# Attention and a mixture of experts on one core: the last second-turn expert is picked on the chip, and half of the final layer norm moves in among the last expert slots

## The chip, the cores and the metric

The kernel runs on one core of a Trainium2 chip. The metric is the time of one execution on the device in microseconds (us). The kernel before the change was timed three times; the median is compared.

## The reference

Input `x` is 4 x 1024 x 256 in float32. Two layers follow each other, each with a residual and a layer norm without weights:

```python
x = layernorm(x + attention(x))      # 16 heads of 16, causal, latent projections, rope
x = layernorm(x + x_moe)             # written out below, x_moe = experts' output plus x
```

The second layer sends every token to 2 of 8 experts:

```python
scores = (x @ router_w.T + router_b) / temp          # per token, 8 experts
gates = sinkhorn(scores, iters=3)                    # over experts, then over the tokens of one element
topk_gates, topk_idx = top_k(gates, 2)               # gates divided by their sum
out_e = (relu(x @ wg[e]) * (x @ wp[e])) @ wo[e]      # 256 -> 512 -> 256
x_moe = x + sum over the two experts of gate * out_e
```

The Sinkhorn step normalizes over the tokens of one element of the batch, so routing can go element by element. There are 4 x 1024 x 2 = 8192 pairs of a token and an expert, on average 1024 to an expert.

## The kernel before

**Attention and routing.** The four elements of the batch are attended one after the other. While element `b` is attended, `finish(b - 1)` makes the first layer norm of the element before and writes its rows to two tensors in DRAM: `x1_rows`, from which the experts gather, and `results`, onto which the experts' outputs are added. `route(b - 1)` (L682) then works out the gates, the two experts of each token, and the place of each pair. Each expert has a region of `REGION` rows in the DRAM tensor `pairs`; `base` (one column for each expert) holds where the next pair of each goes, and grows with every element routed (L824). `scatter` (L839) writes the pairs there by indirect DMAs. `lay_out` (L863) works out, after the last element, which expert has pairs beyond the first 1024, and so what the further slots work on.

**Expert slots.** Experts work in slots of up to 512 pairs (`ER`). `first` holds one slot for each expert, pairs 0 to 511 of its region. They take pairs of the first three elements alone, so that they can run while the last element is finished and routed. `second` holds one slot for each expert, pairs 512 to 1023, in reverse order of the experts. The first of these has `like` set to the last of the first turn (L1102): the same expert, so it takes over its split weights. `further` are slots of 256 pairs (`SR`) for what is left; which expert and which rows they work on is a value in SBUF that SP loads into a register (`value`, L904). `SURE = 3` of them always run; if more are filled, the rest run in a conditional block (L1223).

**One slot.** `pairs_of` (L931) loads the list of pairs, `gather` (L950) the rows of x by four indirect DMAs on GpSimd (two for a further slot), `weights` (L961) the three matrices of 512 KB on SP's queue, `halves` (L975) splits each matrix into a high and a low part (cast on ScalarE, subtraction on VectorE, two of each for a matrix), and `rows` (L986) transposes the gathered rows on PE and splits them. `slot` (L995) then does, for each of four blocks of the 512 hidden columns, the two products on PE (three passes each, for the split), relu on ScalarE, the product on VectorE, and its split. After that come the products with `wo`, for each 128 pairs one output block `eo`, which ScalarE scales by the gate (L1026) and GpSimd adds onto `results` by an indirect DMA (L1027). There are 6 buffers for `eo`. The adds of one slot wait until those of the slot before have landed, since both may touch a row. `begin` (L1191) prepares the slot after while one runs: list and gather of the slot after next, rows and splits of the next one, weights of the slot after next.

A scheduler orders the instructions of each engine when the kernel is built, by priority and by a simulated timeline. On the chip each engine works its queue in that order.

**The final layer norm.** It stands behind the last slot. SP loads `results` back in eight chunks `z` of 512 rows (L1240). For each, VectorE takes the statistics (L1254, L1255), GpSimd makes scale and offset (L1257 to L1261), and then ScalarE scales the first five (L1264) and VectorE the last three (`DZ = 3`, L1272). SP stores (L1243).

## Time and profile before

| | us |
|---|---|
| median of three runs | 1103.58 |
| lowest and highest of them | 1100.23 and 1110.93 |
| the profiled execution | 1094.58 |
| its span, first to last instruction | 1092.8 |

Busy time in the profiled execution: PE (matmul) 978.1 us, VectorE 733.1, ScalarE 625.0, GpSimd 474.4. In the profile's names, PE is TensorE, DVE VectorE, ACT ScalarE, POOL GpSimd and SP SyncE. L1027 is line 1027 of the kernel before. A line of a group gives engine, line, operation, what it writes and reads, and the count. "Idle before" is the time in which the engine stood still ahead of an instruction, with what released it. The profile's rows have the duration of an indirect DMA on POOL as the time that POOL is held, not the transfer's.

### The profile page before, as it was taken

How to read it: one execution, taken by the hardware profiler on the slowest of the kernel's cores; microseconds unless marked ns; L12 is line 12 of the kernel's file. 1: busy time of each engine (PE TensorE's matmuls, PEld its weight loads, DVE VectorE, ACT ScalarE, POOL GpSimd, SP SyncE). 2: the span in 40 equal slices, each digit the busy share in tenths (PEclk: the TensorE clock that was granted, in tenths of full speed). 3: DMA queues.
4: the chain of work that ended last, by engine and by line, in shares of the span. 5: the costliest groups of instructions: out<-in, count | busy, mean ns of one | idle time of the engine just before them, and what ended most of it. 6: DMA issues, size and time to landing. Idle time of an engine off the chain costs nothing.

```text
span 1092.8 us, 18055 instructions
## 1 busy us (share of the span) xinstructions
PE 978.1 (90%) x6436; PEld 609.1 (56%) x6436; DVE 733.1 (67%) x1622; ACT 625.0 (57%) x1314; POOL 474.4 (43%) x543
## 2 busy tenths in 40 slices
PE   6689999999999999998989996899999699999960
PEld 4555433455535355543444343478888488888860
DVE  4767787888888778677648882266675354655636
ACT  3445766766665655675556663675654355655633
POOL 6267511122443531452233216425566864654535
PEclk9889999999999999999989999899999799999995
DMA  6673420231240330333243320256563555655647
GB/s 248 182 213 103 117 96 23 63 116 52 76 121 24 100 117 3 126 82 86 58 102 84 57 71 2 80 168 162 120 169 69 128 99 137 151 144 114 148 62 308
DMA packets 71363, 119.67 MB, mean 110 GB/s; under 512 B 16416, under 2 KB 43040, under 8 KB 70880
## 3 DMA queue, kind: packets, MB, share of 16 engines
q1 hardware_dynamic: 48544, 81.76, 24.4%
q0 software_dynamic: 20672, 36.41, 15.3%
q8 instruction: 53, 0.87, 0.3%
q10 hardware_dynamic: 2048, 0.27, 0.2%
q14 instruction: 46, 0.38, 0.1%
HBM read 82.52 MB, written 35.60 MB: 108 GB/s over the span
## 4 chain that ended last, share of the span: by engine, by line
PE 76%; DVE 6%; ACT 6%; DMA 5%; issue 2%; SPq 2%; another core or an unknown queue 2%; POOL 1%; ACTq 0%; DVEq 0%; POOLq 0%
PE y L435 13%; PE s L351 11%; PE sT L455 11%; PE gp L196 3%; PE gp L197 3%; PE gp L195 3%; PE eo L195 3%; ACT pT L466 3%; PE eo L196 3%; PE eo L197 3%; PE po L622 3%; PE lp L197 2%; PE lp L196 2%; PE lp L195 2%; PE s L368 2%
## 5 line engine op out<-in xcount | busy, mean ns | idle before, releaser
L466 ACT ACTIVATE pT<-sT 128x512 f32<-128x512 f32 (+1 forms) x608 | 326.6, 576 | 183.3 <-PE sT L455 124.3
L372 DVE TENSOR_REDUCE mx<-s 128x1 f32<-128x384 f32 (+3 forms) x352 | 216.8, 633 | 43.0 <-PE s L368 36.8
L455 PE MATMUL sT<-qs,ks 98*128 98x512 bf16 (+3 forms) x768 | 216.2, 330 | 27.2 <-ACT pT L466 20.6
L351 PE MATMUL s<-ks,qs 96*128 96x512 bf16 (+3 forms) x768 | 211.9, 333 | 17.1 <-DMA ks<-parts 7.0
L381 DVE TENSOR_REDUCE mx<-s 128x1 f32<-128x512 f32 x256 | 171.4, 682 | 42.6 <-PE s L351 38.8
L473 POOL TENSOR_SCALAR_AFFINE_SELECT pT<-pT 128x512 f32<-128x512 f32 x112 | 70.5, 636 | 298.0 <-ACT pT L466 293.5
L435 PE MATMUL y<-pT,va 128*32 128x512 f32 (+3 forms) x1536 | 169.9, 502 | 2.0 <-POOL pT L473 1.3
L1027 POOL DMA_INDIRECT results<-eo,ents x64 | 104.2, 1629 | 88.2 <-ACT eo L1026 73.1
L351 PEld LDWEIGHTS <-qs 96*128 96x128 bf16 x768 | 70.9, 100 | 117.0 <-issue 89.9
L455 PEld LDWEIGHTS <-ks 98*128 98x128 bf16 x768 | 69.7, 99 | 93.1 <-issue 60.1
L195 PE MATMUL eo<-wh,hh 128*128 128x256 f32 x280 | 81.4, 292 | 7.8 <-ACT eo L1026 7.8
L189 DVE TENSOR_TENSOR wl<-w,wh 128x512 fp32r<-128x512 f32 x108 | 69.7, 684 | 27.0 <-ACT wh L188 19.3
L368 PE MATMUL s<-mask,ident_b 128*128 128x128 bf16 (+2 forms) x352 | 87.0, 248 | 0.0
L1010 DVE TENSOR_TENSOR relu<-relu,lp 128x512 f32<-128x512 f32 x64 | 43.7, 684 | 61.5 <-ACT relu L1009 21.9
L953 POOL DMA_INDIRECT xg<-x_rows,ents x64 | 65.4, 1022 | 32.8 <-issue 17.3
L196 PE MATMUL eo<-wl,hh 128*128 128x256 f32 x280 | 79.5, 285 | 0.0
L1009 ACT ACTIVATE relu<-gp 128x512 f32<-128x512 f32 (+1 forms) x76 | 42.8, 563 | 61.7 <-PE gp L197 30.8
L197 PE MATMUL eo<-wh,hl 128*128 128x256 f32 x280 | 77.8, 284 | 0.0
L845 POOL DMA_INDIRECT pairs<-ent,so_i x64 | 66.1, 1033 | 19.3 <-issue 17.6
L189 DVE TENSOR_TENSOR hl<-relu,hh 128x512 fp32r<-128x512 f32 (+1 forms) x76 | 48.5, 645 | 28.7 <-ACT hh L188 20.3
L435 PEld LDWEIGHTS y<-pT,va 128*32 128x32 f32 x1536 | 31.9, 108 | 63.3 <-issue 48.0
L195 PE MATMUL gp<-xh,wh 128*128 128x512 f32 (+1 forms) x176 | 64.3, 372 | 2.9 <-DVE relu L1010 1.8
(213 smaller groups left out, 1862.5 us busy)
## 6 DMA issues: line engine op xcount, KB each, us to landing
ks<-parts SPq DMA_DIRECT2D x90, 128.0 KB
w<-in_wg_dram SPq DMA_DIRECT2D x18, 512.0 KB
w<-in_wp_dram SPq DMA_DIRECT2D x18, 512.0 KB
w<-in_wo_dram SPq DMA_DIRECT2D x18, 512.0 KB
qs<-parts SPq DMA_DIRECT2D x66, 128.0 KB
parts<-lv POOLq DMA_DIRECT2D x12, 384.0 KB
parts<-lv POOLq DMA_DIRECT2D x24, 192.0 KB
xh<-in_x_t_dram SPq DMA_DIRECT2D x8, 512.0 KB
```

Of the source, the lines that this page charges most:

```text
L189: (sub or nc.vector).tensor_tensor(lo, src, hi.bitcast(F32), ALU.subtract)
L195: nc.tensor.matmul(ps, lhsT=sh, rhs=mh, start=(i == 0), stop=False)
L196: nc.tensor.matmul(ps, lhsT=sh, rhs=ml, start=False, stop=False)
L197: nc.tensor.matmul(ps, lhsT=sl, rhs=mh, start=False, stop=(i == n - 1))
L351: nc.tensor.matmul(ps, lhsT=q(h, half)[:NROW, t * P : (t + 1) * P], rhs=k(h, kc)[:NROW, :w], start=first, stop=last,)
L368: nc.tensor.matmul(each[:, :, w - P :], lhsT=ident_b, rhs=mask.unsqueeze(1).to_broadcast([P, m, P]), start=False, stop=True,)
L372: nc.vector.tensor_reduce(mx_of[:, half, h0 : h0 + m, t], each, AX.X, ALU.max)
L381: nc.vector.tensor_reduce(mx_of[:, kc, h, t : t + 1], ps, AX.X, ALU.max)
L435: nc.tensor.matmul(acc[g, qc][SLOT * h : SLOT * (h + 1), lo:], lhsT=va[b % 2][:, kb, at : at + SLOT], rhs=pT[:, h, lo:], start=(kb == 0), ...
L455: nc.tensor.matmul(st[:, h % m * w : (h % m + 1) * w], lhsT=k(h, kb // BPQ)[: NROW + 2, kb % BPQ * P : (kb % BPQ + 1) * P], rhs=q(h, qc)[: ...
L466: nc.scalar.activation(pT[:, h + 1 - m : h + 1, lo:], st[:, : m * w].rearrange("p (h t) -> p h t", t=w), AF.Exp, scale=scale,)
L1027: ins = nc.gpsimd.indirect_dma_start(out=results[:, :], out_offset=bass.IndirectOffsetOnAxis(ap=k.ent[:, j, 1:2], axis=0), in_=eo, in_offs ...
```

## The change

- In the routing of the second element, `order_of_second` finds the expert that has the fewest pairs of the first two elements (the lowest number among equals). The second turn runs round the experts so that this one comes last. Its slots take list and weights by registers, as the further slots do. The sharing of weights between the last first and the first second slot goes.
- The mean over the experts of pairs of the first two elements is 512, so the fewest is at most 512, and the last second slot holds none of them. When the slot before it has been added, the rows of these two elements are final, unless some expert has over 1024 pairs of them. For that case `again` raises `filled`, and the conditional block also does the norm of these rows over.
- `load_early` puts the loads of the first four chunks of z on GpSimd's queue, ahead of the output products of the last second slot. Their layer norm is issued behind the last split (`mark`) of the three further slots: two chunks, one, and one. They use buffers of the attention that are free by then.
- Behind the last slot stand chunks 4 to 7. Two of them are scaled on ScalarE and two on VectorE (`DZ = 2`).

```diff
-DZ = 3
+DZ = 2
...
+    EARLY = B // 2
...
         nc.vector.tensor_tensor(base, base, ps[:, NE : NE + E], ALU.add)
+        if b == EARLY - 1:
+            order_of_second()
...
+    def order_of_second():
+        few = tab("few", [E])
+        nc.vector.tensor_tensor(few, floor[:1], base[:1], ALU.subtract)
+        most, again = tab("most", [1]), tab("again", [1])
+        nc.vector.tensor_reduce(most, few, AX.X, ALU.min)
+        nc.vector.tensor_scalar(again, most, -float(ER), float(NOVER), ALU.is_lt, ALU.mult)
+        tables["again"] = again
+        nc.vector.tensor_reduce(most, few, AX.X, ALU.max)
+        nc.vector.tensor_scalar(few, few, most, None, ALU.is_equal)
+        nc.vector.tensor_tensor(few, few, rank[:1], ALU.mult)
+        nc.vector.tensor_reduce(most, few, AX.X, ALU.max)
+        seq = tab("seq", [2, E])
+        seqi = tables["second"] = small.tile([1, 2, E], I32, tag="seqi", name="seqi", bufs=1)
+        nc.vector.tensor_scalar(seq[:, 0], slot_no[:, :E], most, float(E + 1), ALU.subtract, ALU.add)
+        nc.vector.tensor_copy(seqi[:, 0], seq[:, 0])
+        nc.vector.tensor_single_scalar(seqi[:, 0], seqi[:, 0], E - 1, ALU.bitwise_and)
+        nc.vector.tensor_copy(seq[:, 0], seqi[:, 0])
+        nc.vector.tensor_scalar(seq[:, 1], seq[:, 0], float(REGION), float(ER), ALU.mult, ALU.add)
+        nc.vector.tensor_copy(seqi[:, 1], seq[:, 1])
...
     def pairs_of(k):
-        if k.which == 2:
-            row = value(1, k.s, NLIST - SR)
+        if k.which:
+            row = value(k.table, 1, k.s, NLIST - k.rows)
...
     def weights(k, i):
-        if k.like is not None:
-            return
-        if k.which == 2:
+        if k.which:
             if i == 0:
-                k.e = value(0, k.s, E - 1)
+                k.e = value(k.table, 0, k.s, E - 1)
...
     def halves(k, i):
-        if k.like is not None:
-            k.hl[i] = k.like.hl[i]
-            return
...
-            split(hh, hlo, r)
+            k.mark = split(hh, hlo, r)
             hs.append((hh, hlo))
             next(between, None)
+        if ahead is not None:
+            ahead()
...
-    second = [Slot(1, e) for e in reversed(range(E))]
-    second[0].like = first[-1]
+    second = [Slot(1, n) for n in range(E)]
...
+    n_early = EARLY * T // QC
+    early_z = {}
+    def load_early():
+        for i in range(n_early):
+            z = work.tile([P, T], F32, tag="yT0", name=f"ze{i}", bufs=2) if i < 2 else work.tile(
+                [P, BPQ, C], F32, tag="x1", name=f"ze{i}", bufs=X1_BUFS
+            )
+            z = early_z[i] = z.rearrange("p (n c) -> p n c", c=C) if i < 2 else z
+            with tc.issue_after(further[0].gathered.ins):
+                ins = nc.gpsimd.dma_start(out=z, in_=rows_of(results, i))
+            for o in added:
+                after(ins, o)
+
+    def run(keys, given=(), ahead={}, behind={}):
         drain(begin(keys, 0, given))
         for n, key in enumerate(keys):
-            slot(key, begin(keys, n + 1, given))
-    run(first + second + further[:SURE], (0,))
+            slot(key, begin(keys, n + 1, given), ahead.get(n))
+            for i in behind.get(n, ()):
+                with tc.issue_after(key.mark.ins):
+                    by_scalar(i, early_z[i], "e")
+
+    keys = first + second + further[:SURE]
+    n = keys.index(second[-1])
+    run(keys, (0,), {n: load_early}, {n + 1: (0, 1), n + 2: (2,), n + 3: range(3, n_early)})
...
-    for i in range(n_z):
-        load_z(i)
+    for i in range(n_early, n_z):
+        zs[i] = zp.tile([P, BPQ, C], F32, tag="z", name=f"z{i}", bufs=n_z - n_early)
+        nc.sync.dma_start(out=zs[i], in_=rows_of(results, i))
+    for i in range(n_early, n_z):
         if i < n_z - DZ:
-            for j in range(BPQ):
-                nc.scalar.activation(
-                    z[:, j, :], z[:, j, :], AF.Identity, bias=off[:, j : j + 1], scale=rstd[:, j : j + 1]
-                )
-            store_z(i, z)
+            by_scalar(i, zs[i], "f")
         else:
-            rest.append((i, z, rstd, off))
+            rest.append((i, zs[i], *norm_z(i, zs[i], "f")))
```

`by_scalar` and `norm_z` hold the same instructions as the loop of the final norm before: statistics, GpSimd's scale and offset, four activations, a store.

## The prediction

> **What bounds the kernel now.** I read the page for the share of each engine, then the windows of the last 230 us, then the rows behind the last expert, then SP's and POOL's rows.
>
> ```profile
> PE 978.1 (90%) x6436; PEld 609.1 (56%) x6436; DVE 733.1 (67%) x1622; ACT 625.0 (57%) x1314; POOL 474.4 (43%) x543
> ...
> PE   6689999999999999998989996899999699999960
> ...
> DMA  6673420231240330333243320256563555655647
> ```
>
> The page: PE is busy 90% of the span, and of its 40 slices (27.3 us each, in tenths) only the last is empty, with the DMA engines at seven tenths there.
>
> ```profile
> core 0: us, PE busy (x) PEld busy (x) DVE busy (x) ACT busy (x) POOL busy (x), PEclk, DMA share, GB/s
> 895.00:1038.00 143.00, 141.00 (x855) 124.41 (x854) 81.82 (x135) 83.49 (x168) 77.25 (x59) 1.00 0.59 138
> 1038.00:1058.00 20.00, 19.09 (x158) 18.68 (x156) 9.00 (x22) 10.04 (x26) 7.97 (x5) 1.00 0.42 66
> 1058.00:1067.00 9.00, 0.00 (x0) 0.00 (x0) 0.00 (x0) 0.16 (x1) 3.08 (x2) 0.69 0.33 40
> 1067.00:1093.00 26.00, 0.00 (x0) 0.00 (x0) 17.04 (x76) 10.04 (x20) 13.70 (x32) 0.50 0.83 323
> ```
>
> The windows (length, busy us with counts, granted clock, DMA share, GB/s) show two bounds. In the second turn of the experts, 895 to 1038 us, PE is busy 141.0 of 143 us, VectorE and ScalarE 82 and 83; in the further slots, to 1058, PE has 19.1 of 20 and the others half. Then PE has nothing: the last adds land, and 26 us of final layer norm follow.
>
> ```profile
> 1067.04 4.08 SPq L1240 DMA_DIRECT2D z<-results  x8
> 1070.39 1.41 DVE L1254 BATCH_NORM_STATS2 bnst_f<-z 128x6 f32<-128x256 f32 x4 [15.98 <-DMA z<-results]
> ...
> 1072.49 1.04 POOL L1258 TENSOR_TENSOR rstd_f<-rstd_f,neg_half 128x4 f32<-128x4 f32 x1
> ...
> 1074.18 2.07 ACT L1264 ACTIVATE z<-z,off_f,rstd_f 128x256 f32<-128x256 f32 x4 [16.02 <-POOL off_f L1261]
> ...
> 1087.98 1.38 DVE L1272 TENSOR_SCALAR z<-z,rstd_f,off_f 128x256 f32<-128x256 f32 x4 [0.67 <-POOL off_f L1261]
> ```
>
> These rows of the end are merged by line. A z chunk costs VectorE 1.57 us (four statistics of 0.41 us, their aggregates between), GpSimd 1.9 us (1.04 for the power at L1258), and 2.07 us on ScalarE or 1.38 us on VectorE to scale. GpSimd does its eight from 1072.17 to 1087.94 without a gap, and sets the end: the last store is issued at 1089.4, the span ends at 1092.8.
>
> **The change part by part.** The profiled execution took 1094.58 us (1.8 around its span), 9.0 below the median of the runs, 1103.58. The sum is made against 1094.58 and carried to the median.
>
> *1. The tail.* Four chunks stand behind the last add in place of eight. Statistics begin at 1070.4, 1072.0, 1074.1 and 1075.7, as the first four did; the fourth's end at 1077.3, GpSimd has its offset at 1080.2 as now, VectorE scales until 1081.6 (1.38), and the last store takes its 3.4 us: 1085.0. **Gain 7.8 us**; 6.5 if the fourth load lands a chunk's 1.3 us later, 9 if the last store is quicker with half as many ahead of it.
>
> *2. The order, worked out on the chip.* Thirteen small VectorE instructions in the routing of the second element (its base update ran at 509.3), one more in the layout. The layout's own rows take 0.14 to 0.16 us and start 0.19 apart in a chain: 2.5 us. Near 509 PE was busy 8.7 to 10.0 of 10 us, VectorE 5.0 to 8.6, which hides most. 0 to 2.5; I take 0.5, near the free end because VectorE has gaps.
>
> *3. Fresh weights for the first second slot*, which shared the split weights of the last first slot: 1.5 MB, 6 casts of 0.62 us on ScalarE (3.7), 6 subtractions of 0.69 us on VectorE (4.1). Between 863 and 895 these engines were busy 14.8 and 15.0 of 32 us: 0, and 4.1 without that cover.
>
> *4. Lists and weights by a register.* Eight DMAs, with register loads on SP, in place of one. The further slots work so already:
>
> ```profile
> 1007.62 0.38 SPq L973 DMA_DIRECT2D w<-in_wo_dram  x1
> 1008.58 0.35 SPq L935 DMA_DIRECT2D ent<-pairs  x1
> ...
> 1021.82 0.37 SPq L973 DMA_DIRECT2D w<-in_wo_dram  x1
> 1023.01 0.35 SPq L935 DMA_DIRECT2D ent<-pairs  x1
> ```
>
> SP's rows: the list (L935) of the second and third further slot goes out 1.0 and 1.2 us behind the wo weights (L973) of the slot before, which wait until VectorE has split the previous ones. The first went out at 852.93, so I take it that what uses a register keeps its place on SP.
>
> ```profile
> 1020.23 1.55 POOL L1027 DMA_INDIRECT results<-eo,ents  x1 [1.16 <-ACT eo L1026]
> 1026.83 1.01 POOL L953 DMA_INDIRECT xg<-x_rows,ent  x1 [5.04 <-DMA ent<-pairs]
> ...
> 1029.42 1.65 POOL L1027 DMA_INDIRECT results<-eo,ents  x1 [0.30 <-ACT hh L188]
> ...
> 1037.91 1.89 POOL L1027 DMA_INDIRECT results<-eo,ents  x1 [0.30 <-ACT xh L188]
> 1044.00 1.54 POOL L1027 DMA_INDIRECT results<-eo,ent  x1 [4.19 <-ACT wh L188]
> 1045.84 1.54 POOL L1027 DMA_INDIRECT results<-eo,ent  x1 [0.30 <-ACT relu L1009]
> ...
> 1059.79 1.54 POOL L1027 DMA_INDIRECT results<-eo,ent  x1 [3.14 <-DMA results<-eo,ent]
> ```
>
> POOL's rows: the third's gather (L953) stood 5.04 us idle for its list, an add (L1027) behind it. In the second turn wo weights went out at 950.5 and 971.86, gathers at 951.83 and 971.76; 5.2 us behind the weights, as in the further slots (1007.62 to 1012.99 and 1021.82 to 1026.83), they come 4 and 5 us late, and the adds behind them move from 959.43 and 976.86 to 960.9 and 982.3. Six output buffers against four adds to a slot of 17.9 us leave half a slot, 9 us, until PE waits; the gathered rows are needed a slot later. At the turn itself weights went out at 859.07, 860.27 and 864.46; now they are the first second slot's, its list follows near 866 and its gathers near 870, for transposes that stood at 877.98. 0 to 4 us there, and to 10 us in all if eight slots lose the 1.25 us by which PE fell short from 1020 to 1038 (16.75 of 18). I take 1, near the free end because the buffers cover 9.
>
> *5. Early loads*: four of 512 KB on POOL, after the 15th slot's adds, the last begun at 1020.23 and landed 3.9 us later as the chain of waits has it: 1024.1. A 512 KB transfer took POOL 0.83 us (L650), four 3.3: 1027.5. Behind them stand the last gather (needed at 1039.9) and the 16th slot's adds, which write the same tensor and must wait for the landing. 2 MB beside 1 MB of weights at the tail's 320 GB/s is 9.4 us: 1033.5, with latency 1034.5. Then four adds of 1.85 us, landed at 1044.3; two, landed at 1050.3; two at 1051.03 and 1055.11, when their data exist, as before. **0**: the loads may land until 1038.5 before the end moves. Beyond it, each us late is one us; 3 is a bound, with part 6's offsets in the same queue.
>
> The Trainium skill (DMA: Bandwidth & Descriptors, Issuing engine by pattern) speaks against the place: it gives simple loads to Sync, as generally faster. The trace agrees for the issue, 0.83 us on POOL against 0.37 to 0.43 on SP; by SP the sum would still be 0 here.
>
> *6. Early norms in the further slots*: VectorE 4 x 1.57 = 6.3, ScalarE 4 x 2.07 = 8.3, GpSimd 4 x 1.9 = 7.6 us. From 1036 to 1058 they were idle 12.0, 10.2 and 12.4 of 22 us. It fits in sum, but two chunks come where the second further slot's relu and casts want ScalarE, and an activation that waits for POOL's offsets blocks all behind it. 0 to 8.3; I take 2, near the free end because the idle time exceeds the work.
>
> Sum: -7.8 + 0.5 + 0 + 1 + 0 + 2 = -4.3, 1090.3 for the profiled execution and **1099.3** for the median. A measurement of this kernel tells about 1%, 11 us, from no change: its three runs lie 10.7 us apart.
>
> **The rivals.**
>
> *A. Faster by more than the tail.* Four gathers, 5.2 us of POOL, stood at 854.77 between adds, where PE had 22.6 of 33 us (830 to 863). Their list now comes later; if those adds go ahead of them, PE's hole may close by 5.2 us, and with parts 2 to 6 at nothing: -13, 1090.6. For it: POOL is busy 26.3 of those 33 us. Against: the output activation that ended PE's stall of 7.2 us, at 856.73, ran before the adds behind the gathers.
>
> *B. Slower: the list behind the weights.* If gathers stay ahead of adds on POOL and come over 9 us late, the buffers run out and PE waits in every slot; 9 us is where it decides, and I found 4 to 5. At 3 us for each of eight slots, 24 - 7.8 = +16: 1119.8. For it: the 5.04 us idle. Against: PE lost 1.25 us there.
>
> *C. The gain is eaten.* Parts 5 and 6 at their bounds, 3 and 8.3, with 0.5 and 1 of parts 2 and 4: -7.8 + 12.8 = +5, 1108.6. For it: ScalarE's spare is 10.2 against 8.3. Against: offsets take POOL 1.9 us, and it has gaps of 4.
>
> *D. The order isn't what it says.* Over 1024 early pairs of one expert would have the norms done again. Counted from the reference's inputs, the first two elements give 476, 472, 478, 516, 533, 481, 598 and 542; the least is under the 512 of the first turn. Chance nothing; it would cost a second pass of the four chunks, 1107.
>
> **How the numbers follow.** Forecast 0.43, A 0.28, B 0.15, C 0.14. The forecast's own range is 1094.6 to 1107.6 (-9 to +4). The range, 1088 to 1113, takes in A and C and leaves out B. Faster by over 1% is A, 0.28; slower is B with a little of C, 0.17; within 1% the rest, 0.55.
>
> **What would show it.** Right: z loads on POOL near 1024, the 16th slot's adds from 1034, four chunks and some 18.5 us behind the last landing in place of 26.4, PE still at 141 of 143. Wrong: long idle of gathers for lists and PE waiting on eo (B), relu behind waiting z activations (C), PE busy near 850 (A).

## The result, and the profile after

The changed kernel takes 1118.46 us (median; 1117.88 to 1122.86), the kernel before 1106.77 beside it (1100.23 to 1111.62): a ratio of 1.0116, 95% interval 1.0074 to 1.0157. **It is slower by about 12.8 us by the ratio (the medians lie 11.7 apart); forecast was 4.3 us faster.** The profiled execution took 1117.99 us, with a span of 1116.2. The profiled execution of before, 1094.58 us, is shorter than all six of its timed runs, so the two spans are not subtracted from each other below; stretches of them are.

The page of the profile after, the row of busy time and PE's row of the 40 slices (27.9 us each, in tenths):

```profile
PE 993.2 (89%) x6436; PEld 615.2 (55%) x6436; DVE 735.9 (66%) x1638; ACT 629.0 (56%) x1324; POOL 479.3 (43%) x547
...
PE   6689999999999999989899996899997899999850
```

PE's last slices were 9, 6 and 0; now they are 8, 5 and 0. The layer norm left the end, and PE is idle in its place. The windows (length, busy us with counts, granted clock, DMA share, GB/s) say where:

```profile
core 0: us, PE busy (x) PEld busy (x) DVE busy (x) ACT busy (x) POOL busy (x), PEclk, DMA share, GB/s
917.00:1023.00 106.00, 105.26 (x617) 91.08 (x616) 59.46 (x94) 60.88 (x120) 58.99 (x45) 1.00 0.64 147
...
1052.00:1098.00 46.00, 22.49 (x143) 21.06 (x143) 12.44 (x44) 17.01 (x41) 23.46 (x26) 0.75 0.38 79
1098.00:1116.00 18.00, 0.00 (x0) 0.00 (x0) 9.14 (x40) 4.15 (x8) 6.89 (x16) 0.50 0.61 234
```

In the second turn PE is as busy as before (105.26 of 106 us). From 1052 on, in the further slots and the wait behind them, it has 22.49 of 46 us, and no other engine is full either: they wait for one another. Then 18 us of layer norm follow instead of 26. The tail's loads:

```profile
1098.08 1.76 SPq L1318 DMA_DIRECT2D z<-results  x4
```

The first load goes out at 1098.08 and the span ends at 1116.2: 18.1 us, against 25.8 (1067.04 to 1092.8). The gain of part 1 is there, and more than all of it is spent before 1098.

**The early loads.** GpSimd's rows from the last add of the 15th slot on:

```profile
1033.67 3.28 POOL L1052 DMA_INDIRECT results<-eo,ent  x1 [1.25 <-ACT eo L1051]
1042.35 2.24 POOL L1283 DMA_DIRECT2D ze<-results  x4 [5.40 <-DMA results<-eo,ent]
...
1053.07 1.62 POOL L1052 DMA_INDIRECT results<-eo,ent  x1 [4.50 <-DMA ze<-results]
```

The add held GpSimd 3.28 us (1.55 before) and its landing let the loads go at 1042.35, 8.7 us after its start. The loads landed 10.7 us later, and only then could the 16th slot's adds begin (4.50 us idle for `ze`).

**The early norms.** Rows of GpSimd, ScalarE and PE in the further slots:

```profile
1059.86 1.04 POOL L1257 TENSOR_SCALAR rstd_e<-mv_e 128x4 f32<-128x4 f32 x1
1060.98 1.05 POOL L1258 TENSOR_TENSOR rstd_e<-rstd_e,neg_half 128x4 f32<-128x4 f32 x1
1063.43 1.63 POOL L1052 DMA_INDIRECT results<-eo,ent  x1 [1.40 <-DMA results<-eo,ent]
1064.54 0.77 POOL L1260 TENSOR_TENSOR off_e<-mv_e,rstd_e 128x4 f32<-128x4 f32 x1
1065.39 0.25 POOL L1261 TENSOR_SCALAR off_e<-off_e 128x4 f32<-128x4 f32 x1
...
1065.68 2.07 ACT L1267 ACTIVATE ze<-ze,off_e,rstd_e 128x256 f32<-128x256 f32 x4 [5.42 <-POOL off_e L1261]
...
1089.15 2.07 ACT L1267 ACTIVATE ze<-ze,off_e,rstd_e 128x256 f32<-128x256 f32 x4 [7.37 <-POOL off_e L1261]
...
1068.10 0.50 PE L197 MATMUL eo<-wh,hh 128*128 128x256 f32 x1 [2.80 <-ACT hh L190]
```

This is a chain over three engines. An add stands between the power (L1258) and the offset (L1260) of the first chunk on GpSimd's queue, and waits there for adds to land. ScalarE's scaling waits 5.42 us for that offset. Behind the scaling on ScalarE's queue stands the cast `hh`, and PE waits 2.80 us for it. The last chunk shows the same at the end: 7.37 us, behind the last slot's adds.

### The profile page after: what moved, and what is told of

Its sections match the earlier page's. It is cut to its first block, busy times and chain, and to the rows that moved or that the text cites. A ratio compares the mean times of both kernels' runs of the same rounds, so it can differ in the third digit from the quotient of the medians.

```text
span 1116.2 us, 18174 instructions
## 1 busy us (share of the span) xinstructions
PE 993.2 (89%) x6436; PEld 615.2 (55%) x6436; DVE 735.9 (66%) x1638; ACT 629.0 (56%) x1324; POOL 479.3 (43%) x547
## 3 DMA queue, kind: packets, MB, share of 16 engines
q0 software_dynamic: 21248, 38.50, 15.8%
## 5 line engine op out<-in xcount | busy, mean ns | idle before, releaser
L457 PE MATMUL sT<-qs,ks 98*128 98x512 bf16 (+3 forms) x768 | 218.1, 334 | 26.4 <-ACT pT L468 15.3
L437 PE MATMUL y<-pT,va 128*32 128x512 f32 (+3 forms) x1536 | 172.8, 510 | 2.4 <-POOL pT L475 1.3
L191 DVE TENSOR_TENSOR wl<-w,wh 128x512 fp32r<-128x512 f32 x114 | 73.5, 684 | 27.9 <-ACT wh L190 18.5
L1052 POOL DMA_INDIRECT results<-eo,ent x38 | 63.1, 1661 | 44.4 <-ACT eo L1051 19.9
L1052 POOL DMA_INDIRECT results<-eo,ents x32 | 53.6, 1674 | 43.4 <-ACT eo L1051 26.9
L190 ACT CAST wh<-w 128x512 fp32r<-128x512 f32 x114 | 63.8, 618 | 7.3 <-PE gp L198 2.3
```

The costliest lines, as they stand in the source:

```text
L191: return (sub or nc.vector).tensor_tensor(lo, src, hi.bitcast(F32), ALU.subtract)
L437: nc.tensor.matmul(acc[g, qc][SLOT * h : SLOT * (h + 1), lo:], lhsT=va[b % 2][:, kb, at : at + SLOT], rhs=pT[:, h, lo:], start=(kb == 0), ...
L457: nc.tensor.matmul(st[:, h % m * w : (h % m + 1) * w], lhsT=k(h, kb // BPQ)[: NROW + 2, kb % BPQ * P : (kb % BPQ + 1) * P], rhs=q(h, qc)[: ...
L1052: ins = nc.gpsimd.indirect_dma_start(out=results[:, :], out_offset=bass.IndirectOffsetOnAxis(ap=k.ent[:, j, 1:2], axis=0), in_=eo, in_offs ...
```

## The experiments

Kernels of one lot ran on one chip, and each ratio is to the kernel before on that chip. Before takes 1099 us on the first lot's chip, and 1060 to 1063 on those of the other four. In two profiles of before, of 1093.8 and 1061.4 us, some 25 of the 32 us between them stand ahead of the first slot's gather (701.6 and 676.8), and nearly all of the rest ahead of the second turn; why chips differ so stays open.

All profiles are cut at the same four points: start of the last add of the 15th slot, start of the last add, first load of the tail, end of the span. This is the table to keep in view:

| kernel | 15th slot's last add to last add | to the tail's loads | to the end | sum | ratio (95% interval) |
|---|---|---|---|---|---|
| before (four profiles) | 40.8 to 41.4 | 5.4 | 25.8 to 26.0 | 72.0 to 72.6 | 1 |
| after (first result) | 53.55 | 10.86 | 18.1 | 82.5 | 1.0116 (1.0074 to 1.0157) |
| after, third lot | 52.85 | 10.68 | 18.2 | 81.8 | 1.0171 (1.0141 to 1.0201) |
| order alone, first lot | 37.2 | 5.84 | 26.15 | 69.2 | 0.9999 (0.9965 to 1.0032) |
| order alone, third lot | 37.4 | 5.95 | 26.2 | 69.6 | 1.0075 (1.005 to 1.010) |
| order alone, fourth lot | 37.6 | 5.70 | 26.15 | 69.5 | 1.0070 (1.0045 to 1.0095) |
| norms behind the last slot | 44.8 | 18.02 | 18.1 | 81.0 | 1.0141 (1.0107 to 1.0176) |
| adds free of the loads | 50.1 | 10.71 | 18.1 | 79.0 | 1.0064 (1.0036 to 1.0093) |
| stores late | 51.9 | 5.49 | 21.2 | 78.6 | 1.0146 (1.010 to 1.0193) |
| adds free, scaling late | 45.7 | 7.33 | 19.9 | 73.0 | 1.0102 (1.0066 to 1.0138) |
| adds free, loads alone | 40.5 | 6.90 | 19.8 | 67.2 | 1.0039 (1.0013 to 1.0064) |
| loads alone | 42.1 | 5.60 | 20.0 | 67.6 | 1.0065 (1.0037 to 1.0093) |
| order, rows first | 40.9 | 5.48 | 26.4 | 72.8 | 1.0060 (1.0033 to 1.0086) |
| loads alone, rows first | 41.9 | 5.58 | 19.7 | 67.2 | 1.0027 (1.0006 to 1.0049) |
| fixed order, loads alone | 42.0 | 5.53 | 20.1 | 67.6 | 0.9957 (0.9930 to 0.9984) |
| fixed order, two norms | 43.9 | 9.60 | 20.45 | 73.9 | 0.9974 (0.9951 to 0.9997) |

The first cut moves with the gathers of the second turn. The 15th slot's last add starts 12.5 us behind the first relu of the 16th slot in the kernels with the order, and 8.8 to 8.9 us behind it in the kernel before, with rows first, and with the fixed order. From that relu to the last add it is 49.6 to 50.2 us in the kernel before and 49.7 to 50.1 with the order alone, so their 37.4 us in place of 41 are no gain. So kernels with the order are compared with the order alone (69.4), those with rows first with "order, rows first" (72.8), and those with the fixed order with before (72.0).

### First lot: the order, the norms, the wait for the loads

The kernel before, run again as it was:

> The kernel before, unchanged, to see which stage of it varies: its first profile had 1092.8 us of span, while its six timed runs have a median of 1106.77. If the 6.7 us by which the attention ran longer in the changed kernel (gather of the first slot at 695.6 against 702.3 us) are variation, this profile has that gather near 702 and a span near 1102; if they are the change's, it stays near 696 and the span grows elsewhere. The ratio should be 1.000.

1.0008 (0.9976 to 1.0039). Its first gather stands at 701.6 us, so the changed kernel's later gather is variation; its span is 1093.8 all the same, not 1102.

**The order alone** (parts 2 to 4):

```diff
-DZ = 2
+DZ = 3
...
-    n_early = EARLY * T // QC
+    n_early = 0
...
-    run(keys, (0,), {n: load_early}, {n + 1: (0, 1), n + 2: (2,), n + 3: range(3, n_early)})
+    run(keys, (0,))
```

> Only the order by registers, with the shared weights gone; all eight chunks of the final norm stand at the end again (three scaled on VectorE). Theory 1 (the further slots and the late norm lose the time): this costs only the 6 us by which the first second slot came late behind the pair scatters, 1112 us, ratio 1.005, and the second turn itself is as long as before. Rival (the lists behind the weights lose it in every slot): 1120 us or more, ratio 1.013 and up, with the second turn longer.

0.9999 (0.9965 to 1.0032), under what both theories had. Lists by registers do not stall the slots of the second turn. On this chip no price of the order shows; the third lot says otherwise.

**Norms behind the last split of the last slot**, all four:

```diff
-    ... {n + 1: (0, 1), n + 2: (2,), n + 3: range(3, n_early)})
+    ... {n + 3: range(n_early)})
```

> The changed kernel with its early loads in place, but all four early norms issued behind the last split of the last further slot, so that ScalarE waits for no offsets inside the slots. Theory 1: PE's 10.7 us of lateness in the further slots shrink to 3 or less, and the time to some 1111 us (four norms now stand behind the last slot and partly show). Rival (the adds that wait for the early loads hold the slots up): PE stays 8 us or more late and the time stays at 1118 or rises.

The slots lose 8.7 us less than in the changed kernel (44.8 against 53.55), but the tail's loads come 18 us behind the last add: the last early store now goes out late, and the loads stand behind it. The time, 1.0141, is nearer the rival's, but not for the rival's reason alone.

**Adds that do not wait for the early loads** (they touch other rows):

```diff
             for o in added:
                 after(ins, o)
+            for o in early_ins:
+                tc.declare_no_dep(ins.ins, o.ins, reason="they touch rows of their own")
...
+            early_ins.append(ins)      # in load_early
```

> The changed kernel, but the adds from the last second slot on are declared apart from the early loads (they touch other rows), so no add waits for a load. Theory 1 (ScalarE blocked behind GpSimd's offsets): the adds move up by some 10 us at the last second slot, the further slots gain 3 to 6 us, 1113 us. Rival (the wait for the loads is the whole loss there): all 12 us of the further slots come back, 1106 us.

1.0064: with scaling and offsets left in the slots, the last add is still 50.1 us behind the first cut. That is 3.4 us less than in the changed kernel, as theory 1 had it. (The 1106 us that it took agree with the rival only by number: the kernel before takes 1099 on this chip.)

### Second lot: the block, the scaling, the loads

**Stores late.** The early chunks are stored behind the tail's loads.

```diff
-                    by_scalar(i, early_z[i], "e")
+                    by_scalar(i, early_z[i], "e", False)     # without its store
...
+    for i in range(n_early):                                 # behind the tail's loads
+        store_z(i, early_z[i])
```

> The changed kernel, but the four early chunks are stored behind the loads of the tail, not in the further slots; their loads, statistics, offsets and scaling stay where they are. Theory 1 (the conditional block waits for what is under way, the early stores too, and the tail's loads stand behind it): in the changed kernel the last early store went out at 1091.25 and the tail's loads at 1098.08, 10.9 us behind the start of the last add, where the kernel before had 5.4. Without the stores the loads come 5 to 7 us behind the last add, the four stores then share the tail with 2 MB of loads and 2 MB of stores (some 1 us), and the time falls by 4 to 5 us: ratio to the kernel before near 1.008. Rival (it is the scaling of the last early chunk on ScalarE that holds the block, and not the store): ScalarE ended it at 1091.2, so the loads stay 9 to 11 us behind the last add, and the ratio stays at 1.011 to 1.014. The last add itself should stay 12 to 13 us later against its stage than before in both.

The place is as theory 1 had it, 5.49 us behind the last add. GpSimd, ScalarE and SP of this kernel:

```profile
1053.19 1.58 POOL L1052 DMA_INDIRECT results<-eo,ent  x1 [0.16 <-issue]
...
1055.12 2.07 ACT L1267 ACTIVATE ze<-ze,off_e,rstd_e 128x256 f32<-128x256 f32 x4 [7.61 <-POOL off_e L1261]
...
1058.67 1.94 SPq L1317 DMA_DIRECT2D z<-results  x4
```

and of the changed kernel, whose tail's loads go out at 1098.08:

```profile
1087.22 1.58 POOL L1052 DMA_INDIRECT results<-eo,ent  x1 [0.16 <-issue]
...
1067.78 23.80 SPq L1247 DMA_DIRECT2D out_dram<-ze  x4
```

Both scale the last early chunk just behind the last add. The one that also stores it ahead of the block has its loads 5.4 us later, so it is the store that delays them, and not the scaling. The rows of the block's line show how (line, engine, operation and count; shortest, median and longest in ns; first and last start in us). First the kernel before, then the changed kernel, then stores late, each with the compare and branch in SP's queue; the changed kernel also with SP's waits right behind its branch:

```profile
L1223 SPq COMPARE_BRANCH  x1: 45/45/45, 1039.2 to 1039.2; - x1
```

```profile
L1301 SPq COMPARE_BRANCH  x1: 50/50/50, 1092.0 to 1092.0; - x1
L1301 SPq EVENT_SEMAPHORE  x9: 17/17/17, 1095.2 to 1097.4; - x9
```

```profile
L1302 SPq COMPARE_BRANCH  x1: 50/50/50, 1014.3 to 1014.3; - x1
```

Every engine has a branch of its own in its own queue. In the kernel before and with stores late SP has its branch behind it 22 and 39 us ahead of the last add. In the changed kernel the last early store stands ahead of the branch in SP's queue; it goes out at 1091.25, when ScalarE has scaled, the branch follows at 1092.0, SP's next row comes 3.2 us later, and the first load at 1098.08. So it is the issue of the store that the branch waits for; whether its landing matters too was not separated. But the tail grew from 18.1 to 21.2 us with 2 MB of stores more in it, and the ratio, 1.0146, stayed high: by the cuts 5.4 us are saved and 3.1 given back, not the 1 us expected.

**Adds free, scaling and stores late**: the norms' statistics and offsets alone remain in the slots.

```diff
-                    by_scalar(i, early_z[i], "e")
+                    early_norm[i] = norm_z(i, early_z[i], "e")
...
+    for i in range(n_early):                   # behind the tail's loads
+        scale_z(i, early_z[i], *early_norm[i])
```

> The changed kernel with two edits: adds behind the early loads do not wait for them, and of the early norms only statistics and offsets run in the further slots; scaling on ScalarE and the four stores stand behind the loads of the tail. Theory 1 (in the further slots it is ScalarE's waiting for GpSimd's offsets that blocks the casts and relus behind, and then the block waits for the stores): the last add is 2 to 4 us later against its stage than in the kernel before (9 with scaling in the slots), the tail's loads come 5 to 7 us behind it, the tail takes 18 to 19.5 us in place of 25.8, and the ratio is 0.995 to 1.000. Rival (the statistics on VectorE and the offsets on GpSimd cost the slots just as much, since splits and adds stand behind them): the last add is 6 to 9 us later, and the ratio is 1.001 to 1.004.

The rival is the nearer one. The slots have 45.7 us: 4.4 fewer than with scaling (50.1), but still 5.3 more than with no norms (40.5, the next run). So the scaling on ScalarE was under half of the norms' price. (The run with scaling is of the first lot, where the loads went out 9.1 us behind the 15th slot's last add in place of 5.7 to 5.8; some of the 4.4 may be due to that.) The tail's loads come 7.33 us behind the last add: here GpSimd's last offset stands behind it, and GpSimd's branch behind that.

**Adds free, loads alone**, and **loads alone**: every chunk is normed behind the block (`DZ = 3`). The second is the same with adds that wait for the loads.

```diff
-                with tc.issue_after(key.mark.ins):
-                    by_scalar(i, early_z[i], "e")
...
+    zs.update(early_z)
-    for i in range(n_early, n_z):
+    for i in range(n_z):
```

> The changed kernel with adds that do not wait for the early loads, and nothing of the early chunks but their loads ahead of the conditional block: all eight chunks are normed behind it (three scaled by VectorE, as before). Theory 1 (the early loads cost little once adds do not wait for them; the norms cost the slots their 9 us): the last add is 0 to 1.5 us later against its stage than in the kernel before, the tail's loads come 5.4 to 6 us behind it, and GpSimd's eight chunks of 1.93 us begin some 3.5 us earlier against those loads, so the tail takes 22 to 23 us in place of 25.8: ratio 0.996 to 0.999. Rival (2 MB of loads beside the weights and the gathers delay the slots by themselves): last add 3 to 6 us later, ratio 1.000 to 1.004.

> As the run with only the loads early, but with the adds of the 16th slot waiting for the early loads, as in the changed kernel: the price of that wait alone, with no norms beside it. Theory 1: 3 to 4 us more than the run without the wait: last add 3 to 5 us later against its stage than before, ratio 0.999 to 1.002. Rival (the wait costs only because offsets and adds of the early norms stand in the same queue): the same as the run without the wait within 1 us.

The loads cost the slots 3.1 us (40.5 against 37.4), the wait for them 1.6 more (42.1; by the ratios, whose intervals overlap, 0.26% or 2.8 us), and the tail falls by 6.3 to 20 us, lower than expected: VectorE has passed its own branch by then, and starts the statistics of early chunks while GpSimd still adds. Both should have beaten the order alone by 2 us, and so the kernel before; both were slower. That put the order under suspicion.

### Third lot: the order again

> The kernel before, unchanged, for its own stages on the chip on which the other three of this lot run. On a chip on which it takes 1063 us the two kernels whose early chunks were loaded early and normed late took 4 and 7 us more than before, though the rows from the 15th slot's last add to the end promised -1 and -1. Theory 1: the attention and the first turn differ from chip to chip by the granted clock, and nothing behind 895 us does: last add to the tail's loads 5.4 us, loads to the end 25.8, and second turn with further slots (the 16th gather group's row to the last add) as in the first profile within 1 us. Rival: behind 895 us the kernel before is itself some 4 us shorter on another chip.

> The order of the second turn worked out on the chip, with its lists and weights by register and fresh weights for its first slot, and no early loads or norms: the same kernel as in the first lot, where it took 0.9999 of the time before. Theory 1 (the order costs nothing anywhere): 0.997 to 1.003. Rival (the order costs 4 to 5 us which the first lot's chip hid, and with it the kernels with early loads alone are above before): 1.003 to 1.006.

> The changed kernel, unchanged, on the chip of this lot. Theory 1 (its loss stands in the further slots and at the conditional block and so does not hang on the clock of the attention): +11 to +14 us, ratio 1.010 to 1.014. Rival (the loss differs from chip to chip): outside of that.

The kernel before repeats itself (1.0004, 0.9979 to 1.003), and from the 15th slot's last add on it is as in its first profile, 72.0 us against 72.6. On this chip the order alone costs 0.75%, 8 us (1.0075), more than even the rival had, and the changed kernel 1.0171, which is the rival. The two medians, 1068.36 and 1080.52, lie 12.2 us apart; the cuts give 81.8 - 69.6 = 12.2.

Where it costs shows in a window of 35 us round the end of the last element's scatters, from 10 us ahead to 25 us behind. The kernel before and the order alone, each in its own window, in the first lot:

```profile
846.60:881.60 35.00, 27.61 (x147) 23.07 (x146) 13.79 (x22) 13.63 (x26) 27.11 (x23) 0.90 0.46 100
```

```profile
842.90:877.90 35.00, 28.48 (x146) 23.38 (x144) 15.30 (x24) 14.17 (x27) 25.96 (x22) 0.90 0.43 95
```

and in the fourth:

```profile
816.10:851.10 35.00, 31.52 (x167) 26.86 (x166) 16.05 (x25) 15.61 (x31) 25.05 (x23) 0.90 0.49 104
```

```profile
815.70:850.70 35.00, 27.55 (x145) 23.12 (x144) 17.18 (x27) 15.97 (x30) 25.26 (x22) 0.91 0.47 93
```

With the order PE has 27.6 to 28.5 of 35 us on either chip. Before has 27.6 on one, where PE waits 5.84 us for an output buffer, and 31.5 on the other, where it waits 2.42. The third lot's chip is like the fourth's (31.53 and 28.31). So on these three chips the price goes with how much the kernel before idles there anyway: 3 to 4 us of PE in this window where it idles 3.5, and none where it idles 7.4. From the end of the scatters to the last add the order adds 5.8 us in the fourth lot (207.5 against 201.8) and 2.9 in the first (208.7 against 205.8), where the ratio's interval, 3.6 us to either side of none, doesn't tell it. In the fourth lot 0.6 us more stand behind the last add; the rest of the ratio's 7.4 us was not located. Why the kernel before idles more on one chip than on the other stays open.

**Offset on VectorE** is an edit of the kernel before alone, for a claim of the prediction: that GpSimd sets the end of the tail.

```diff
-        nc.gpsimd.tensor_tensor(off, mv[:, :, 0], rstd, ALU.mult)
-        nc.gpsimd.tensor_scalar(off, off, -1.0, None, ALU.mult)
+        nc.vector.scalar_tensor_tensor(off, mv[:, :, 0], -1.0, rstd, ALU.mult, ALU.mult)   # a chunk later
```

> The kernel before with one change in the tail alone: the offset of a chunk (two GpSimd instructions, 0.20 and 0.23 us and the gaps) is one VectorE instruction behind the statistics of the next chunk; GpSimd keeps the power. Theory 1 (GpSimd's 1.9 us for each of eight chunks set the end of the tail): GpSimd needs 1.4 us a chunk, VectorE's 1.7 become the bound, the last offset comes 2 to 3 us earlier, and the tail takes 23 to 24 us in place of 25.8: ratio 0.997 to 0.998. Rival (the transfers, 8 MB at 323 GB/s, set the end): the same within 1 us, 0.999 to 1.001.

1.0014 (0.9995 to 1.0032): no gain, and its tail takes 27.2 us against 25.8. GpSimd now stands idle 2.54 and 1.58 us in it for VectorE's statistics. So GpSimd's work alone does not set the end; but the edit also moves every offset behind the statistics of the next chunk, and what sets the end in its place was not separated.

### Fourth lot: the gathers at the turn

GpSimd's queue had two groups of four gathers with four adds between them; with the order it has four adds and then eight gathers. **Rows first** issues list and gathers of the second turn's first slot one slot earlier, which restores the old order of the queue:

```diff
-        early_next = nxt is not None and (nxt.which == 0 or k.which > 0)
+        early_next = nxt is not None
-        if n not in given and (k.which and (n == 0 or not keys[n - 1].which)):
+        if n not in given and k.which and n == 0:
```

> The kernel before, unchanged, for its profile on this lot's chip: where the queue of gathers and adds on GpSimd leaves TensorE idle at the turn from the first turn of the experts to the second. Theory 1 (the price of the order hangs on how much TensorE idles there anyway): with a time near 1060 us some 4 us idle, with a time near 1100 us some 8 to 11.

> The order by registers alone, as in the first and the third lot (0.9999 and 1.0075). Theory 1 (eight gathers in one group behind the sixth slot's adds cost 5 to 8 us where the kernel before idles little at the turn, and nothing where it idles 8 to 11 us): 1.005 to 1.010 on a chip on which the kernel before takes about 1060 us, 0.997 to 1.003 where it takes about 1100. Rival (chance from build to build): anything between.

> The order by registers alone, with the list and the gathers of the second turn's first slot issued one slot earlier in the program, so that GpSimd has them ahead of the sixth slot's adds, as in the kernel before. Theory 1 (the place of those gathers is the whole price of the order): 0.997 to 1.002, whatever the chip. Rival (registers or fresh weights cost it): the same as the order alone, 1.005 to 1.010 on a chip on which the kernel before takes about 1060 us.

The control repeats the price (1.0070), and rows first does not take it away (1.0060): theory 1 fell. What PE waits for has changed, though. Order alone, a row of PE at the turn:

```profile
844.03 0.34 PE L1015 MATMUL xgT_ps<-ident,xg 128*128 128x128 f32 x1 [5.00 <-DMA xg<-x_rows,ent]
```

Rows first, SP, ScalarE and PE:

```profile
830.52 0.38 SPq L963 DMA_DIRECT2D ent<-pairs  x1
831.41 0.38 SPq L999 DMA_DIRECT2D w<-in_wg_dram  x1
...
836.81 1.14 ACT L190 CAST wh<-w 128x512 fp32r<-128x512 f32 x2 [10.49 <-DMA w<-in_wg_dram]
...
838.48 0.79 PE L197 MATMUL gp<-xh,wh 128*128 128x512 f32 x1 [7.87 <-ACT xh L190]
```

With the gathers late, PE waits 5.00 us for rows. With them early, the list stands ahead of weights on SP's queue, where it waits for the scatters to end; the weights go out 0.9 us behind it, ScalarE waits 10.49 us for them, and PE 7.87 for ScalarE. The window has 27.13 of 35 us, as with the order alone. Either way the turn now needs a list, rows and weights right behind the scatters.

**Rows first with the early loads**, adds free of them:

> The early loads alone, with adds that do not wait for them and all norms behind the conditional block (1.0039 in the second lot), and with the gathers of the second turn's first slot ahead of the sixth slot's adds. Theory 1 (the early loads cost 3 us in the further slots and save 4 to 5 in the tail, and the rest of the 1.0039 was the place of the gathers): 0.996 to 1.000. Rival (the loads themselves cost it): 1.003 to 1.005.

1.0027. Theory 1 missed again for the same reason: the order's price is still in it. Against rows first alone it is 0.33% less, about 3.5 us (the intervals overlap; the medians lie 4.8 apart), the worth of the early loads.

### Fifth lot: the loads without the order

**Fixed order, loads alone**: the kernel before's order, one list, and shared weights, with the early loads and adds that do not wait for them. Expert 0 comes last there; it has 476 pairs of the first two elements, under 512. The flag for a second pass is kept and asks for expert 0.

```diff
-    second = [Slot(1, n) for n in range(E)]
+    second = [Slot(1, e) for e in reversed(range(E))]
+    second[0].like = first[-1]
...
```

**Fixed order, two norms** adds statistics and offsets of two early chunks between the last add and the block:

```diff
+    with tc.issue_after(keys[-1].mark.ins), tc.issue_after(added[-1].ins):
+        for i in range(2):
+            early_norm[i] = norm_z(i, early_z[i], "e")
```

> The kernel before, with its fixed order (expert 0 last, whose first two elements give 476 pairs, under the first turn's 512), its one list and the shared weights of the second turn's first slot; added are the early loads, with adds that do not wait for them, and the flag for a second pass; all eight chunks are normed behind the conditional block. Theory 1 (the order costs 5 to 8 us at the turn, the loads cost 3 us in the further slots and save 4 to 5 in the tail): ratio 0.995 to 0.999. Rival (the loads themselves cost what the runs with loads alone lost): 1.003 to 1.005.

> As the run with the fixed order and early loads, with statistics and offsets of two early chunks between the last add and the conditional block, where GpSimd was idle for 4.9 us; scaling and stores stay behind the block. Theory 1 (GpSimd's eight chunks of 1.93 us set the end, and two of them leave the tail): 3 to 4 us less than that run, ratio 0.992 to 0.996. Rival (the block waits for these norms too, or the transfers set the end): 0 to 2 us more than that run.

The first is **faster than both kernels**: 0.9957 (0.9930 to 0.9984), some 4.6 us below before; the cuts give 72.0 - 67.6 = 4.4. Its window at the turn:

```profile
822.60:857.60 35.00, 32.80 (x180) 27.90 (x179) 16.12 (x26) 16.07 (x31) 26.28 (x22) 0.95 0.49 112
```

PE has 32.80 of 35 us: with the order gone, its price is gone. (This chip has no profile of before; on the third and fourth lot's chips before has 31.5.) Last add and tail's loads of this kernel, and then those of the one with two norms, which also has their last offset:

```profile
1035.31 1.54 POOL L1050 DMA_INDIRECT results<-eo,ent  x1 [0.30 <-DVE bnst_f L1255]
...
1040.85 1.77 SPq L1314 DMA_DIRECT2D z<-results  x4
```

```profile
1028.92 1.54 POOL L1050 DMA_INDIRECT results<-eo,ent  x1 [0.30 <-issue]
...
1033.35 0.43 POOL L1263 TENSOR_SCALAR off_e<-off_e 128x4 f32<-128x4 f32 x2
...
1038.52 1.77 SPq L1322 DMA_DIRECT2D z<-results  x4
```

With two norms ahead of the block the loads come 9.6 us behind the last add, not 5.5. No store stands there, and SP's branch is long done (1006.8). This time it is GpSimd's own branch:

```profile
L1306 POOLq COMPARE_BRANCH  x1: 57/57/57, 1033.9 to 1033.9; - x1
L1306 POOLq EVENT_SEMAPHORE  x5: 17/43/43, 1036.6 to 1036.9; - x5
```

It follows the offsets at 1033.9, GpSimd's next row comes 2.7 us later, and SP's loads behind that; without norms it ran at 1034.3, ahead of the last add. So the rival holds: the loads wait for norms too. By the ratios the two runs lie 0.17%, 1.8 us, apart, with intervals that overlap. (The cuts put them 6.3 apart; the profile with norms is shorter ahead of the first cut, by more than that.)

## Why the prediction was wrong, step by step

By the cuts, against the order alone (37.4, 5.8, 26.2), the changed kernel (53.2, 10.8, 18.2, the mean of two profiles) has +15.8 us in the slots, +5.0 to the tail's loads and -8.0 in the tail: +12.8, and the order's own 0 to 8 on top. The first result's 12.8 leaves nothing for the order, the third lot's 18 leaves 5. The sum of the prediction was -4.3.

- **Part 1, the tail: right.** -7.8 was forecast. It is 18.1 and 18.2 us in the two profiles of the changed kernel against 25.8, so -7.6. The reason given, that GpSimd sets the end, was not borne out: an edit that took its offsets off GpSimd gained nothing (1.0014), though that edit also made offsets later.
- **The term that is missing: what stands ahead of the conditional block's branches.** The prediction counted the early stores and offsets as work beside other work. But the tail's loads stand behind the branches of SP and GpSimd, and the last store and the last offset ahead of them: 10.86 us from the last add in place of 5.4. This is +5 us, shown by the run with late stores (5.49) and, for GpSimd's offsets without stores, by that with two norms (9.60). Profile and code of before held it: the If at L1223 stands between the last slot and the loads of L1240.
- **Part 6, the early norms: 2 was taken out of 0 to 8.3; it is about 10.** In the second lot they cost 9.8 us with the adds' wait (stores late 51.9, loads alone 42.1). Without it they cost 50.1 - 40.5 = 9.6, and the changed kernel has 53.2 - 42.1 = 11.1, but in these two differences the loads also went out some 3 us later in the kernel with norms. The bound was ScalarE's work alone, as if the idle times of three engines could be filled one by one. But each chunk is a chain from VectorE to GpSimd to ScalarE, and on each of the three it stands ahead of what PE needs next. Statistics and offsets, which the prediction did not price, have 5.3 of it within one lot; at most 4.4 go with the scaling, the step that it named.
- **Part 5, the early loads: 0 was taken, with a bound of 3; it is 4.7** (42.1 - 37.4). The transfer was sized well: 10.4 us forecast from issue to landing (1024.1 to 1034.5), 10.7 measured in the changed kernel and 11.6 with loads alone. Two terms ahead of it failed. The 15th slot's last add was left at its old place, 8.8 us behind the first relu of the 16th slot, but the order (part 4) moves it to 12.5. And its landing was taken as 3.9 us; it took 5.75 us with loads alone and 8.7 in the changed kernel. With loads alone the loads landed 29.8 us behind that relu (988.8 to 1018.6), where the sum had 23.1 and the end was said to stand still up to 27.1. They were 2.7 us over and cost 4.7, so that room was some 2 us too wide as well. With adds that do not wait 3.1 of the 4.7 remain: PE then waits 1.9 us for rows of the last gather, which stands behind the loads in GpSimd's queue, and the rest is open. With rows first and with the fixed order 0.9 and 1.2 remain (41.9 against 40.9, 42.0 against 40.8).
- **Parts 2 to 4, the order: +1.5 was taken, 0 to 10 and a part-3 bound of 4.1 allowed.** By the ratios it is 0 on the first lot's chip and 7 to 8 us on two others. The steady slots are as forecast: 105.26 of 106 us busy, and lists 1.2 us behind the `wo` weights with 5.42 us of idle time for a gather, as in the further slots before. SP's and GpSimd's rows:

```profile
1014.30 0.37 SPq L999 DMA_DIRECT2D w<-in_wo_dram  x1
1015.50 0.35 SPq L963 DMA_DIRECT2D ent<-pairs  x1
...
1019.70 1.01 POOL L980 DMA_INDIRECT xg<-x_rows,ent  x1 [5.42 <-DMA ent<-pairs]
```

What failed is the turn, "gathers near 870, for transposes that stood at 877.98": there the rows are late, or the weights. Part 3 was priced at 0 by engines' idle time; its transfer, behind a list that waits in SP's queue for the scatters, was not priced.

**The rivals.** C was the right mechanism in part: ScalarE waits for GpSimd's offsets behind waiting adds, but that has at most 4.4 of the 8.3 us that C put there; it had neither the branches nor statistics and offsets in the slots nor the loads' full delay. B's place was wrong, since PE does not wait in every slot; its cause, late lists, cost at the turn on some chips. A half came: on the first result's chip the adds went ahead of the gathers and PE's window at the turn rose from 24.34 to 29.10 of 35 us, but the gain was spent later. D did not occur.

## What to carry to other kernels

Idle time on three engines is not room for a chain that crosses all three: each step stands in an engine's queue ahead of what the bounding engine needs next, so price the chain's longest wait at each crossing, not the sum of its work. Whatever is moved ahead of a conditional block can hold up an engine's branch there; find the engine whose queue comes to its branch last, and see whether the moved store or offset stands ahead of it, before counting it as hidden. And when a slot that needed no list or weights at a tight place is made to need both, look at that place's queues by themselves, on more than one chip.

## What the runs showed of the hardware

- The same indirect add of 128 rows took 3.6 to 9.1 us from issue to landing (3.6 the quickest in the changed kernel of the third lot; 9.1 with adds free of the loads, 1030.23 to 1039.37). In the changed kernel three weight loads of 512 KB were issued at 1035.55 to 1037.86, behind the add at 1033.67, and the DMA engines' busy share was 0.38 from 1034 to 1038 and 1.04 from 1038 to 1042.4; in the fixed order with early loads, with weight loads issued at 994.92 and 997.02 behind the add at 993.33 and a share of 0.68, it took 4.5 us. The Trainium skill (DMA: Bandwidth & Descriptors, Issuing engines are not separate DMA queues) says that transfers share the same 16 DMA engines and interleave whichever engine starts them, which fits these rows; no run here moved the weights alone to show that they are the cause.
- With nothing else ahead of the block, 5.4 to 6.0 us pass from the start of the last add to the first load behind it in seven of these kernels, and 6.9 in an eighth. How much of it is the add's landing was not separated. An engine's branch shows where something holds it back to the end: from SP's branch to SP's next row it is 3.2 us in the changed kernel (1092.0 to 1095.2), from GpSimd's to its next 2.7 with two norms (1033.9 to 1036.6).
- A gap on PE is paid for twice where the granted clock falls. In the first profile of before PE was idle from 850.02 to 857.26; the granted clock was 1.00 up to 853 and 0.50 from 854 to 866, when PE worked again, and a product of 128x512 took 0.80 us at 859.88 where one had taken 0.50 at 848.17. The window at the turn has a mean clock of 0.80 there, with 10.7 us idle, and 0.95 in the fixed order with early loads, with 2.2.
